# Two fused layers with sorted experts: gather rows, result loads and the order of the second layer's sequences are changed

## The chip, the core and the metric

One core of a Trainium2 chip. Its five engines run their own in-order instruction streams: TensorE (PE, matmuls and transposes into PSUM), VectorE (DVE), ScalarE (ACT), GpSimd (POOL, which here issues the indirect and the accumulating DMAs) and SyncE (SP, which issues the plain DMAs). Sixteen DMA engines move the data of all queues. The metric is the device time of one execution in microseconds (us), the median of several runs.

## The reference

The input `x` is 8 sequences of 1024 tokens with 256 features (float32). Two layers follow each other:

```python
x = L0_attn_x
xn = _layernorm(x, axis=-1)
x = x + _L0_attn_ref(xn, ...) + _L0_ffn_ref(xn, ...)
xn = _layernorm(x, axis=-1)
x = x + _L1_attn_ref(xn, ...) + _L1_ffn_ref(xn, ...)
return x
```

- `_L0_attn_ref` is a linear recurrence with a 16-wide state for each of 256 channels, then a layer norm, a GELU, a product with `W_out`, plus `b_out`, plus its input `xn`.
- `_L0_ffn_ref` is a shared expert plus the two best of 8 experts for each token, each `silu(x Wg) * (x Wu) Wd`, weighted with the token's two gates.
- `_L1_attn_ref` takes its softmax over an axis of length one, so each token gets the sum of the values of its sequence, times `w_o`.
- `_L1_ffn_ref` is 8 experts with two per token and a capacity of 2048 tokens each, hidden width 1024, ReLU.

The sum that layer 0 hands on is, for each token, `x + xn + b_out + shared expert` (called "the other terms" below), plus the two weighted expert results, plus the projection of the recurrence.

## The kernel before

64 tiles of 128 tokens; eight tiles are a sequence. The tile `y` holds all tokens in SBUF. The kernel is written in a framework that adds the semaphores, gives buffers of a pool in turn, and lets a simulated schedule put each engine's instructions in order: a later instruction of the program may be issued earlier on its engine if it is ready then. A buffer goes to its next user when every instruction that reads it, a DMA too, has finished. There are five stages.

**Stage A (0 to 209 us), the shared expert and the router, by pairs of tiles.** `normal` writes the normalized rows into `xr4` (three buffers of four tiles) and SP copies them twice into the DRAM table `xnd`, once for each of the token's two choices: 8192 x 2 rows of 257 numbers. `both` makes on ACT the channel-major copy `xc` (L588) and, in place, `y = x + xn` (L592). `shared` runs the shared expert and adds it to `y` (L617). For each sequence `fill` writes `b_out` to the DRAM table `base` from SP (L535), and POOL adds `y` to it with an accumulating DMA (L655). `route0` finds the two experts and gates of 16 tiles, and SP writes the gates into column 256 of `xnd` (L528).

**Stage B (209 to 346 us), the plan.** Ranks, block starts, and one-hot matmuls (`find`, `found`) that give for each of 142 columns of 128 rows the row of `xnd` to gather (`choice`) and the row of the result table `yr` to scatter to (`goes`).

**Stage C (346 to 862 us), 71 expert blocks of 256 rows beside the recurrence.** `bring(n)` copies the expert's number on POOL (L787), loads its weights into `wb` (three buffers) from SP, and gathers two times 128 rows into `xb` (three buffers, L792). `widen(n)` transposes them and runs the first two products; `narrow(n)` runs the third, scales by the gate (L811) into `yo` (two buffers of its own) and scatters from POOL into `yr` (L814). On POOL's stream a block's two scatters come before the gathers of three blocks later. `krylov` and `rest` are the recurrence, whose output replaces `y`.

**Stage D (862 to 1160 us), by sequences b = 0 to 7.** `load(b)` brings the sum's other terms from `base` into `hb` with a plain DMA and then adds the two expert results to it with two accumulating DMAs from POOL (L952), for b = 0 with plain loads and VectorE. The loop at L1228 loads b + 2, normalizes and turns b + 1 (`turn`: ACT L190, PE L933, GELU L934), projects b (`project`: PE L992, DVE L999 adds `hb`), and finishes b (`finish`: moments, the root, normalized rows `xs`, transposes L1022 and L1025, the DRAM table `xd`, router logits L1037). Every second sequence `route` ranks 16 tiles (the one-hot products end in L1140). `attend(b)` copies column sums on POOL (L1053, `vb`), multiplies them on PE (L1056), stores `y` to the output, and adds the result with an accumulating DMA from POOL (L1063). Within an engine the stream is in order, so an instruction of `attend` that waits holds back what follows it.

**Stage E (1160 to 2081 us), layer 1's experts.** 32 blocks of gathered rows, two products (L1339, L1357), an accumulating scatter to the output (L1369). The change does not touch it.

Of the kernel before, what the change touches and what calls it, by code (L numbers as in the profile page):

```python
# [18 lines left out]
P = 128  # L19
# [5 lines left out]
def kernel(  # L25
# [48 lines left out]
    XW = D + 8  # L74
# [11 lines left out]
    base = dram.tile([NTOK, D], F32, name="base")  # L86

    xnd = dram.tile([2 * NTOK, D + 1], F32, name="xnd")
# [128 lines left out]
    with tc.tile_pool(name="xpool", bufs=1) as xpool, tc.tile_pool(name="mo", bufs=2) as mo, tc.tile_pool(  # L217
# [12 lines left out]
        g0 = xpool.tile([P, 2, NT], F32, name="g0")  # L230
        up = xpool.tile([P, NT], F32, name="up")
        off = xpool.tile([P, NT], F32, name="off")
# [5 lines left out]
        choice = xpool.tile([P, NCOL], I32, name="choice")  # L238
        goes = xpool.tile([P, NCOL], I32, name="goes")
# [16 lines left out]
        def hidden(xT, wb, pgu=None):  # L256
# [12 lines left out]
            hh = mo.tile([P, 2 * P], F32, name="hh")  # L269
            nc.vector.tensor_tensor(hh, pgu[:, 0, :], sg, ALU.mult)  # L270
            nc.vector.tensor_tensor(hh, pgu[:, 1, :], hh, ALU.mult)  # L271
            return hh
# [181 lines left out]
        with tc.tile_pool(name="sh", bufs=1) as sh, tc.tile_pool(name="ld", bufs=2) as ld, tc.tile_pool(  # L454
# [5 lines left out]
            scores = sh.tile([P, NT, E], F32, name="scores")  # L460
            cb_t = sh.tile([P, E], F32, name="cb_t")
# [10 lines left out]
            bout_t = sh.tile([P, D], F32, name="bout_t")  # L472
            nc.scalar.dma_start(bout_t, b_out.partition_broadcast(P))
# [6 lines left out]
            nc.vector.tensor_copy(rwT.rearrange("p c e -> p (c e)"), pr[:, : DC * E])  # L480

            def route0(n, tiles):
# [38 lines left out]
                for k in range(2):  # L521
                    wk = rt.tile([P, n, E], F32, name="wk")
                    nc.vector.tensor_tensor(wk, w, hot[k], ALU.mult)
                    nc.vector.tensor_reduce(g0[:, k, tiles], wk, AX.X, ALU.add)
                    mine = xnd[2 * tiles.start * P : 2 * tiles.stop * P, :].rearrange(
                        "(i p k) c -> k p i c", p=P, k=2
                    )[k]
                    nc.sync.dma_start(mine[:, :, D], g0[:, k, tiles])  # L528
# [4 lines left out]
            def fill(b):  # L533

                nc.sync.dma_start(  # L535
                    base[b * S : (b + 1) * S, :].rearrange("(i p) d -> p i d", p=P),
                    bc(bout_t, 1, [P, TPB, D]),
                )

# [16 lines left out]
            def scale(g, mv):  # L556
# [9 lines left out]
                nc.vector.tensor_scalar(up[:, tiles], rstd, 1.0, None, ALU.add)  # L566
# [4 lines left out]
            def normal(i, mv, rstd):  # L571
# [7 lines left out]
                if i % 4 == 3:  # L579
                    for kk in range(2):  # L580
                        mine = xnd[2 * (i - 3) * P : 2 * (i + 1) * P, :].rearrange(
                            "(i p k) c -> k p i c", p=P, k=2
                        )[kk]
                        nc.sync.dma_start(mine[:, :, :D], rows[i // 4])

            def both(i, rstd):
# [4 lines left out]
                )  # L591
                nc.scalar.activation(  # L592
                    y[:, i, :], y[:, i, :], AF.Identity, bias=off[:, i : i + 1], scale=up[:, i : i + 1]
                )

            def shared(i, pr, rstd):
# [16 lines left out]
                for q in range(2):  # L613
                    both(i + q, rstd[:, q : q + 1])
                pgu = ps_k.tile([P, 2, 2 * P], F32, name="pk") if n % 2 else None
                pd = down(hidden(xT, sw, pgu), sw)
                nc.vector.tensor_tensor(y[:, i : i + 2, :], pd, y[:, i : i + 2, :], ALU.add)  # L617
# [9 lines left out]
            for s, g in enumerate(sets):  # L627
# [8 lines left out]
                for k in range(0, len(g), 2):  # L636
# [5 lines left out]
                    if i % TPB == 0:  # L642
                        pr = ps_y.tile([P, TPB, E], F32, name="py")
                        fill(i // TPB)
# [6 lines left out]
                    if i % TPB == TPB - 2:  # L651
# [3 lines left out]
                        nc.gpsimd.dma_start(  # L655
                            base[b * S : (b + 1) * S, :].rearrange("(i p) d -> p i d", p=P),
                            y[:, tiles, :], accum_op=ALU.add,
                        )
# [253 lines left out]
    with tc.tile_pool(name="xr", bufs=3) as xr, tc.tile_pool(name="tr", bufs=1) as tr, tc.tile_pool(  # L912
# [64 lines left out]
        def turn(b):  # L977

            ys = y[:, b * TPB : (b + 1) * TPB, :]
            if b:  # L980
                normalize_act(ys, ys, *scaled[b], TPB)
# [430 lines left out]
```

## Time and profile before

| what | value |
|---|---|
| runs shown | 2085.64, 2090.27, 2096.55 us; median 2090.27 |
| the profiled execution | 2092.45 us, of which its span is 2090.8 us |
| PE busy | 1858.0 us, 89% of the span |
| DVE, ACT, POOL busy | 696.9, 717.8, 677.9 us |
| mean granted TensorE clock | 0.939 of full |
| moved by DMA | 233.16 MB, mean 112 GB/s |

The span runs from the first to the last instruction. "Busy" is the time in which an engine had an instruction running; a matmul's end is modelled by the profiler, so PE's busy time includes overlap and is not PE at its peak. The "DMA share" of a stretch is the busy share of the 16 DMA engines, and can pass 1 where packets overlap. A wait is put down to the engine or DMA whose signal came last.

### The profile page before, as it was taken

Reading aid. Unit: us, or ns where it says so; the run is one execution under the profiler, and the core shown is the slowest. Engines: PE = TensorE matmul, PEld = TensorE weight load, DVE = VectorE, ACT = ScalarE, POOL = GpSimd, SP = SyncE. Lnnn points to the kernel's source line nnn. Section 1 sums busy time; section 2 is a strip of 40 time slices with the busy share of each in tenths; the row PEclk is TensorE's granted clock in tenths of the full one; section 3 lists DMA queues with packets and bytes.
Section 4 is the critical chain, followed back from the end, with each engine's and each line's share of the span. In section 5 each row is a group of like instructions: output and inputs, shape, how many; then the busy total and the mean of one; then the engine's idle time right before and its main releaser. Section 6 shows DMA issues by size and latency. Waiting matters only on the chain. (4 is left out here: it accounts for less than half of the span.)

```text
span 2090.8 us, 24217 instructions
## 1 busy us (share of the span) xinstructions
PE 1858.0 (89%) x8619; PEld 1398.3 (67%) x8619; DVE 696.9 (33%) x2093; ACT 717.8 (34%) x1626; POOL 677.9 (32%) x688
## 2 busy tenths in 40 slices
PE   6978798989889897767677899999999999999996
PEld 5867586877777776556565466666666666666664
DVE  6754794444443443535556110100111001011000
ACT  5953352222222221545655222222222222222221
POOL 0000003555555566211110333333333333333322
PEclk9988898999999999888887899999999999999998
DMA  9987214545454555699966223232322222232211
GB/s 275 219 190 179 52 47 120 156 145 165 135 153 135 151 177 157 185 249 178 195 129 157 56 39 79 39 76 36 78 40 59 59 59 54 39 79 38 39 20 20
DMA packets 228888, 233.16 MB, mean 112 GB/s; under 512 B 50904, under 2 KB 203296, under 8 KB 228640
## 3 DMA queue, kind: packets, MB, share of 16 engines
q0 software_dynamic: 69408, 102.87, 25.3%
q1 hardware_dynamic: 156672, 126.35, 21.1%
q10 hardware_dynamic: 2688, 2.40, 0.4%
q8 instruction: 68, 1.11, 0.2%
q14 instruction: 52, 0.43, 0.1%
HBM read 136.87 MB, written 97.85 MB: 112 GB/s over the span
## 5 line engine op out<-in xcount | busy, mean ns | idle before, releaser
L1339 PE MATMUL phe<-xTe,w1t 128*128 128x512 f32 x1024 | 447.5, 595 | 0.6 <-issue 0.6
L1357 PE MATMUL poe<-w2t,hT 128*128 128x256 f32 x2048 | 447.3, 379 | 0.0
L1357 PEld LDWEIGHTS poe<-w2t,hT 128*128 128x128 f32 x2048 | 386.7, 190 | 51.7 <-issue 0.5
L1339 PEld LDWEIGHTS phe<-xTe,w1t 128*128 128x128 f32 x1024 | 195.5, 191 | 233.9 <-issue 230.7
L1369 POOL DMA_INDIRECT out_dram<-yo,invi x128 | 201.7, 1576 | 444.7 <-DMA out_dram<-yo,invi 245.6
L1346 ACT ACTIVATE hT<-phe,b1T 128x512 f32<-128x512 f32 x256 | 176.0, 687 | 248.7 <-PE phe L1339 242.5
L1368 ACT ACTIVATE yo<-yo,gr 128x256 f32<-128x256 f32 x128 | 58.0, 500 | 441.4 <-DVE yo L1364 441.4
L1364 DVE TENSOR_TENSOR yo<-poe,b2t 128x512 f32<-128x512 f32 x64 | 44.3, 692 | 406.6 <-PE poe L1357 400.5
L1308 POOL DMA_INDIRECT xg<-xd,invi x128 | 124.1, 969 | 168.1 <-PE px L1322 129.1
L322 PE MATMUL pk<-kr 128*128 128x129 f32 (+7 forms) x896 | 150.9, 306 | 27.3 <-ACT kr L333 24.4
L1323 DVE COPY xTe<-px 128x512 f32<-128x512 f32 x64 | 41.2, 686 | 383.5 <-PE px L1322 383.5
L814 POOL DMA_INDIRECT yr<-yo,goes x142 | 141.9, 1000 | 77.5 <-DVE yo L811 36.3
L322 PEld LDWEIGHTS pk<-kr 128*128 128x128 f32 x896 | 129.5, 202 | 51.7 <-ACT kr L333 35.7
L263 PE MATMUL pgu<-xT,wb 128*128 128x256 f32 x568 | 147.3, 405 | 13.1 <-ACT xT L253 10.4
L792 POOL DMA_INDIRECT xb<-xnd,choice x142 | 141.1, 993 | 46.9 <-issue 36.0
L263 PEld LDWEIGHTS pgu<-xT,wb 128*128 128x128 f32 x568 | 112.0, 203 | 42.5 <-ACT xT L253 21.9
L333 ACT COPY kr<-pk 128x256 f32<-128x256 f32 x192 | 69.4, 374 | 125.2 <-DVE kr L329 92.7
L268 ACT ACTIVATE sg<-pgu 128x256 f32<-128x256 f32 x87 | 33.4, 384 | 199.1 <-PE pgu L263 154.6
L278 PE MATMUL pd<-wb,hh 128*128 128x256 f32 x284 | 84.5, 412 | 12.2 <-DVE hh L271 12.0
L270 DVE TENSOR_TENSOR hh<-pgu,sg 128x256 f32<-128x256 f32 x87 | 36.8, 423 | 152.0 <-ACT sg L268 123.6
L787 POOL COPY wb<-wrow 1x1 int32<-1x1 int32 x71 | 12.9, 182 | 229.9 <-PE pgu L752 117.8
L811 DVE TENSOR_SCALAR yo<-pd,xb 128x256 f32<-128x256 f32 x142 | 62.4, 478 | 51.9 <-PE pd L278 40.1
(319 smaller groups left out, 2424.7 us busy)
## 6 DMA issues: line engine op xcount, KB each, us to landing
wb<-wpk SPq DMA_DIRECT2D x71, 384.0 KB
xnd<-xr SPq DMA_DIRECT2D x32, 512.0 KB
hk<-kscr SPq DMA_DIRECT2D x32, 512.0 KB
hb<-yr POOLq DMA_DIRECT2D x14, 1024.0 KB
base<-bout_t SPq DMA_DIRECT2D x8, 1024.0 KB
base<-y POOLq DMA_DIRECT2D x8, 1024.0 KB
hb<-base SPq DMA_DIRECT2D x8, 1024.0 KB
w1t<-in_L_ffn_w_dram SPq DMA_DIRECT2D x8, 1024.0 KB
```

Source lines behind the costliest of these rows:

```text
L263: nc.tensor.matmul(pgu[:, j, :], lhsT=gu[:, j, c, :], rhs=xT[:, c, :], start=(c == 0), stop=(c == DC - 1),)
L278: nc.tensor.matmul(pd[:, q, :], lhsT=hh[:, q * P : (q + 1) * P], rhs=wb[:, 2 * DC * I : WW], start=True, stop=True,)
L322: nc.tensor.matmul(pk[:, j, :n], lhsT=t[:, 1 - j, P:], rhs=t[:, j, P - k : P - k + n], start=True, stop=True,)
L333: nc.scalar.copy(t[:, :, P:], pk[:, :, k : k + P])
L792: nc.gpsimd.indirect_dma_start(out=xb[:, q, : D + 1], out_offset=None, in_=xnd[:, :], in_offset=bass.IndirectOffsetOnAxis(ap=choice[:, 2 * ...
L811: nc.vector.tensor_scalar(yo[:, q, :], pd[:, q, :], xb[:, q, D : D + 1], None, ALU.mult)
L814: nc.gpsimd.indirect_dma_start(out=next(yr_own)[:, :], out_offset=bass.IndirectOffsetOnAxis(ap=goes[:, 2 * n + q : 2 * n + q + 1], axis=0) ...
L1308: nc.gpsimd.indirect_dma_start(out=xg[:, q, :], out_offset=None, in_=xd[:, :], in_offset=bass.IndirectOffsetOnAxis(ap=invi[:, q0 + q : q0 ...
L1339: nc.tensor.matmul(ph, lhsT=w1t[:, c, h * P : (h + 1) * P], rhs=xT[:, c], start=(c == 0), stop=(c == DC - 1),)
L1346: nc.scalar.activation(hT[:, h], ph, AF.Relu, bias=b1T[:, e * HC + h : e * HC + h + 1])
L1357: nc.tensor.matmul(po[:, r, :], lhsT=hT[:, h, q + r, :], rhs=w2t[:, h, :], start=(h == 0), stop=(h == HC - 1),)
L1369: nc.gpsimd.indirect_dma_start(out=of[:, :], out_offset=bass.IndirectOffsetOnAxis(ap=invi[:, q0 + r : q0 + r + 1], axis=0), in_=yo[:, r, : ...
```

## The change

- `base`, `fill` and their accumulating DMAs go. `xnd` has one row per token, of 514 numbers: the normalized row, the two gates, and half of the sum's other terms. The halves come from `b_out` and `sw_down` times 0.5, `up` times 0.5 and a new column `offh`. `y = x + xn` moves from ACT (L592) to two VectorE instructions per pair of tiles, and the shared expert's result is added by two VectorE instructions of 256 columns instead of one of 512. SP writes the half rows once per four tiles.
- The gather takes the token's whole row (2056 bytes instead of 1028). A new tile `which` says which of the two gates counts; two small VectorE instructions per block (`gk`, `gs`) select it. `narrow` adds the scaled product to the half row inside `xb` and scatters from there; `yo`'s own buffers go. So both expert results of a token carry one half of the other terms each.
- `load` brings both results with two plain DMAs per sequence into `yk` (three buffers of half a sequence); `project` adds them on VectorE, two instructions per pair of tiles instead of one.
- In stage D the loop runs with a lag: in turn b it projects b, and turns out, ranks and attends b - 1. `vb` is copied on VectorE instead of POOL. The last sequence follows behind the loop in two halves.

```diff
-    base = dram.tile([NTOK, D], F32, name="base")
-    xnd = dram.tile([2 * NTOK, D + 1], F32, name="xnd")
+    xnd = dram.tile([NTOK, XR], F32, name="xnd")          # XR = 2 * D + 2
...
-            nc.vector.tensor_tensor(hh, pgu[:, 0, :], sg, ALU.mult)
-            nc.vector.tensor_tensor(hh, pgu[:, 1, :], hh, ALU.mult)
+            nc.vector.tensor_tensor(sg, pgu[:, 0, :], sg, ALU.mult)
+            nc.vector.tensor_tensor(sg, pgu[:, 1, :], sg, ALU.mult)
...
-                    mine = xnd[...]
-                    nc.sync.dma_start(mine[:, :, D], g0[:, k, tiles])
+                nc.sync.dma_start(token_rows(tiles)[:, :, D : D + 2], g0[:, tiles, :])
...
-                    for kk in range(2):
-                        nc.sync.dma_start(mine[:, :, :D], rows[i // 4])
+                    nc.sync.dma_start(mine[:, :, :D], rows[i // 4])
...
-                nc.scalar.activation(
-                    y[:, i, :], y[:, i, :], AF.Identity, bias=off[:, i : i + 1], scale=up[:, i : i + 1]
-                )
...
-                nc.vector.tensor_tensor(y[:, i : i + 2, :], pd, y[:, i : i + 2, :], ALU.add)
+                for t in range(i, i + 2):
+                    nc.vector.scalar_tensor_tensor(
+                        y[:, t, :], y[:, t, :], up[:, t : t + 1], bhalf, ALU.mult, ALU.add
+                    )
+                pd = down(hh, sw)
+                for q in range(2):
+                    nc.vector.scalar_tensor_tensor(
+                        y[:, i + q, :], pd[:, q, :], offh[:, i + q : i + q + 1], y[:, i + q, :],
+                        ALU.add, ALU.add,
+                    )
+                if i % 4 == 2:
+                    nc.sync.dma_start(
+                        token_rows(slice(i - 2, i + 2))[:, :, D + 2 :], y[:, i - 2 : i + 2, :]
+                    )
...
-                        out=xb[:, q, : D + 1],
+                        out=xb[:, q, :XR],
...
+                gk = mo.tile([P, 2, 2], F32, name="gk")
+                nc.vector.tensor_tensor(
+                    gk, xb[:, :, D : D + 2], which[:, 2 * n : 2 * n + 2, :], ALU.mult
+                )
+                gs = mo.tile([P, 2], F32, name="gs")
+                nc.vector.tensor_reduce(gs, gk, AX.X, ALU.add)
...
-                yo = eb_.tile([P, 2, D], F32, name="yo", bufs=2)
+                yo = xb[:, :, D + 2 : XR]
                 for q in range(2):
-                    nc.vector.tensor_scalar(
-                        yo[:, q, :], pd[:, q, :], xb[:, q, D : D + 1], None, ALU.mult
+                    nc.vector.scalar_tensor_tensor(
+                        yo[:, q, :], pd[:, q, :], gs[:, q : q + 1], yo[:, q, :],
+                        ALU.mult, ALU.add,
                     )
...
-            nc.sync.dma_start(hb, base[toks, :].rearrange("(i p) d -> p i d", p=P))
-                for j in range(2):
-                    nc.gpsimd.dma_start(hb, both[:, :, j, :], accum_op=ALU.add)
+            for t in range(0, TPB, TPB // 2):
+                yk = xr.tile([P, TPB // 2, 2, D], F32, name="yk")
+                nc.sync.dma_start(yk, both[:, t : t + TPB // 2])
+                hold[b].append(yk)
...
-                nc.vector.tensor_tensor(ys[:, t : t + 2, :], po, hb[:, t : t + 2, :], ALU.add)
+                nc.vector.tensor_tensor(two, po, yk[:, :, 0], ALU.add)
+                nc.vector.tensor_tensor(two, two, yk[:, :, 1], ALU.add)
...
-            nc.gpsimd.tensor_copy(vb, bc(colsum[:, :, b], 2, [P, DC, P]))
+            nc.vector.tensor_copy(vb, bc(colsum[:, :, b], 2, [P, DC, P]))
...
         for b in range(NB):
+            project(b)
+            if b + 1 < NB:
+                load(b + 1)
+            nc.sync.dma_start(of[...], y[:, b * TPB : (b + 1) * TPB, :])
+            last = b - 1
+            if b:
+                normal_out(last, whole)
+            if b + 1 < NB:
+                normal_in(b + 1)
+            if b:
+                turn_out(last, whole)
+            if b + 1 < NB:
+                turn(b + 1)
+            if b < NB - 1:
+                measure(b, whole)
+                if b:
+                    logits(last)
+                roots(b)
+            else:
+                measure(b, slice(0, TPB // 2))
+                logits(last)
+            if b:
+                attend(last)
+            if b and last % 2 == 1:
+                ends = route((last - 1) * TPB, 2 * TPB, ends)
```

`normal_out`, `turn_out` and `logits` are the parts of the old `finish`, `normal_in` the first half of the old `turn`; `roots` takes the root and the reciprocals of both norms and starts the moments of sequence b + 3.

## The prediction

> **What bounds the kernel now.** The chain of waits says PE for the end, but follows back only to 1134 us: it shows stage E, 921 us of products without a pause, which the change leaves alone. So I took busy time by stages (us; PE, PEld, DVE, ACT, POOL busy with counts; clock; DMA share; GB/s):
>
> ```profile
> 20.00:72.00 52.00, 50.34 (x314) 45.47 (x314) 39.76 (x168) 48.06 (x105) 1.79 (x1) 1.00 0.96 295
> 72.00:121.00 49.00, 47.86 (x280) 42.11 (x279) 39.02 (x145) 44.09 (x80) 4.66 (x3) 1.00 0.99 208
> 121.00:209.00 88.00, 69.97 (x320) 58.52 (x320) 40.64 (x127) 32.53 (x74) 6.20 (x4) 0.79 0.83 192
> ...
> 346.00:862.00 516.00, 450.58 (x2553) 378.84 (x2551) 219.90 (x642) 134.25 (x352) 289.57 (x348) 0.95 0.49 146
> 862.00:1160.00 298.00, 207.80 (x1107) 168.85 (x1107) 154.84 (x522) 162.29 (x404) 44.38 (x47) 0.81 0.86 190
> 1160.00:2081.00 921.00, 912.32 (x3322) 610.60 (x3322) 90.68 (x160) 233.99 (x384) 319.29 (x250) 0.99 0.26 51
> ```
>
> Stage A starts full on PE and on DMA, then PE thins out. Stage C is 87% PE with POOL at 56%. Stage D has no engine over 70% and a DMA share of 0.86. The waits of stage D (engine and line, whom it waited for, us, times, longest):
>
> ```profile
> POOL hb L952 <- DMA hb<-yr: 83.4, 6, 19.1
> DVE y L999 <- PE pd L992: 58.1, 5, 21.3
> ...
> POOL hb L952 <- DMA hb<-base: 41.4, 4, 18.5
> ```
>
> and POOL's timeline in it (start, duration, then in brackets the idle time before):
>
> ```profile
> 928.02 1.55 POOL L952 DMA_DIRECT2D hb<-yr  x1 [2.73 <-DVE colsum L1045]
> 928.91 1.07 POOL L1053 COPY vb<-colsum 128x256 f32<-128x256 f32 x1
> 949.06 1.55 POOL L952 DMA_DIRECT2D hb<-yr  x1 [19.08 <-DMA hb<-yr]
> ```
>
> Each accumulating load takes 18 to 20 us to land, the second of a sequence waits for the first, and POOL waits in order. So a sequence costs two of them, about 37 us, and 298 / 8 is 37.3: stage D runs at their pace. PE suffers through `vb` (L1053), which stands behind them on POOL: the products of `attend` wait for it, and the next projection waits behind those.
>
> Stage A's late stalls, on PE's timeline:
>
> ```profile
> 150.66 1.10 PE L278 MATMUL pd<-sw,hh 128*128 128x256 f32 x4 [1.21 <-DVE hh L271]
> 158.76 1.22 PE L249 MATMUL pt<-ident,xr 128*128 128x128 f32 x4 [7.00 <-DVE xr L576]
> ```
>
> PE is idle 7 us for normalized rows. DVE makes eight `xr` rows in one burst at 125.8 and six at 158.3, having had gaps up to 7.3 us just before: rows wait for the buffers of `xr4`, and those for their DMAs, in a queue that is full (share 0.96 and 0.99 until 121).
>
> **Stage A, forecast -28 us.** The router's products L606 (8 per pair of tiles) number 72, 90 and 96 in the first three windows: 9, 11 and 12 pairs, at 49 / 11.25 = 4.4 us per pair in the second and 88 / 12 = 7.3 in the third. Removed are 8 fills and 8 accumulating transfers of 1 MB and four of eight gate writes. The second copy of the normalized rows is replaced by the half rows, 16 DMAs of 512 KB for 16. The 45 MB of the stage become 28; the first 121 us alone moved 25. So I expect no DMA stall. Then VectorE counts. Per pair it gains two instructions from SBUF and two from PSUM, 256 wide (0.42 by L576 and L270), and loses one of 0.69 (L617): +1.0 on 39.0 / 11.25 = 3.5, so 4.5, just over PE's pace of 4.4. I take 4.7 per pair. The last 12 pairs gain 12 x 2.6 = 31 and the 11 before them lose 0.3 each: 28 net. ACT loses two of 0.59 (L592) per pair; it is hidden behind PE. Ends: -35 (pace kept at 4.4), -10 (VectorE at 6.2).
>
> **Stage B, nothing.** `found` gains two instructions of 142 columns, under 0.3 us each; the first gathers wait for it, so at most 0.6 us.
>
> **Stage C, forecast +10 us.** Three edits. (1) The gate: 71 x 2 small VectorE instructions of about 0.17 (the smallest rows), 24 us on an engine with 296 us free; if they delayed `narrow`, it would be 0.34 per block. (2) 142 gathers of twice the bytes, +18.7 MB in a stage of half-busy DMA engines. Gathers run three blocks ahead, so a us or two of landing is hidden. (3) The new wait, the one that speaks against the change: the scatter now reads `xb`, so the gather of block n + 3 can be issued only when block n's scatters have landed. Behind it on POOL stand the next expert copy and the next scatters, and through them all later gathers. A block on POOL with no wait:
>
> ```profile
> 616.28 0.18 POOL L787 COPY wb<-wrow 1x1 int32<-1x1 int32 x1
> 616.63 1.01 POOL L814 DMA_INDIRECT yr<-yo,goes  x1 [0.17 <-issue]
> 617.94 0.98 POOL L814 DMA_INDIRECT yr<-yo,goes  x1 [0.30 <-issue]
> 619.23 1.01 POOL L792 DMA_INDIRECT xb<-xnd,choice  x1 [0.30 <-issue]
> 620.54 0.97 POOL L792 DMA_INDIRECT xb<-xnd,choice  x1 [0.30 <-issue]
> ```
>
> That is 5.2 us; with the usual 0.58 after the copy 5.6. The stage needs 516 / 71 = 7.3 per block. The trace's DMA packets tell the landing: the stage's last scatter, undisturbed, was there 1.1 us after its instruction, all 142 in the median 2.0, nine in ten within 2.8. With 2.0 in place of the gap of 0.3 a block is 7.3, exactly the pace. As blocks come unevenly (5.2 to 12.3 us between scatters) and three buffers smooth only part, I take +10. A rule weighs here: the Trainium skill, "DMA: Bandwidth & Descriptors", section "Anatomy of one DMA", gives a fixed 2.0 us per GpSimd DMA, mostly the write's receipt, plus bytes / 436 GB/s; 128 KB make 2.3 from the issue, or 1.3 after the 1.0 of the instruction. By it a block is 6.6 and the wait costs nothing. I follow the row, which has this stage's traffic. Ends: 0, and at 2.8 us 71 x 0.8 = +57.
>
> **Stage D, forecast -47 us.** Gone are 14 accumulating loads from POOL and the loads of `base`; what comes instead is one MB per DMA from SP. The first sequence's plain loads, made today, show the price: 3 MB issued at 861.4 to 863.7 were added up from 870.2 to 875.5, about 4 us per MB. The new loads go out when a half buffer is free, a turn ahead, so they hide; uncovered they would cost 8 us per sequence. On SP they stand behind the store of `xd` and of the router's weights, both of the turn before. POOL keeps only L1063, for which nobody waits until stage E.
>
> What is late next is PE: 207.8 / 8 = 26.0 us per sequence. ACT has 162.3 / 8 = 20.3. DVE has 154.8, less L961 (4.9), plus 32 second adds of 0.69 and eight `vb` copies of 0.4: 175 / 8 = 21.9. The lag lets PE turn b - 1 while b's moments are made, where it now waits (36.3 us in stage D before L1022). Full overlap of three engines so near each other is not to be had: I take 29 per turn. Sum: 5 to the first product (2 MB to load instead of 3), 16 for turn 0 (projection 7.1, moments 6.3, root 2.5), 6 x 29 = 174, 7 for the last projection, 5 for what of sequence 6 now comes behind it (L1037 and L1056), and today's 42 from the last L999 (1119.9) to the first L1339 (1161.8), which still holds the last halves and the routing. That is 249, against 300 today with the same ends; I round the gain of 51 down to 47 for the last loop turn's moments.
>
> The second rule: the Trainium skill, "TensorE: Matmul & The Clock Gate", Part 1, says the clock is gated by default and recent activity releases it. Stage D stands at 0.81. By the rule a denser stage gets 1.00, PE falls to 21 per sequence, VectorE leads, a turn is 25 and the stage gains 24 more. By the row I grant nothing, since PE still pauses in each turn. Ends: -71 and, at a turn of 34, -17.
>
> **Sum.** -28 + 10 - 47 = -65 against the profiled execution's 2092.45 (1.7 beyond its span): 2027.5. That run lies 2.2 above the median of those shown. I write 2028.
>
> **Rivals.**
> 1. The forecast: near 2028; 55%.
> 2. The chain in D goes but another takes its place, at 34 us per turn: SP in order (a half load behind the store of `out`, which waits for the whole projection) or VectorE, which gains 2.5 per sequence and feeds PE in both directions. With A at -12 and C at +10: 2092 - 12 + 10 - 17 = 2073. For it: three engines near 22 to 26 and in-order queues. Against it: none is over 70% today. 21%.
> 3. The other side: the landing in C decides. From 3.0 us a block on POOL is 8.3 and the stage costs 71 x 1.0 = +71, which eats all; at 3.6 it is 8.9 and +114, so 2092 - 28 - 47 + 114 = 2131. For it: POOL's order, the doubled gathers on the same engines, and that one landing in ten is already 2.8. Against it: the median, and that the schedule may put the next scatter before the gather. 18%.
> 4. The traffic is less and the stalls stay (A's wait for rows is not the queue but the order on SP, D's loads collide with the stores): within 0.5% of 2090; 6%.
>
> Differences within 0.5%, some 10 us, can't be told from no change here. Faster: cases 1 and 2, 0.76. Same: 0.06. Slower: 0.18. The range runs from 1985 (A -35, C 0, D -71) to 2095, which leaves case 3 out.
>
> **What would show it.** Right: no L952 on POOL and `pd` starting every 27 to 31 us in D; in A PE's gaps for `xr` gone and the last router product near 180; in C two us of idle POOL before the gathers and a stage of about 525. Wrong: POOL idle 3 us or more there with a stage over 570 (case 3); D over 280 with PE waiting for `yk` or for VectorE (case 2); A still with bursts of `xr`.

## The result, and the profile after

The changed kernel is slower. Its time is 2149.06 us (median of 4 runs, 2139.66 to 2152.03) against 2091.16 of the kernel before on the same chip (4 runs): ratio 1.027, 95% interval 1.023 to 1.031. The profiled execution has a span of 2145.1 us against 2090.8, so the two profiles differ by 54.3 us. To see where, I cut both by the same events: the end of the last router product (A), the first scatter (B), the last scatter (C), the first product of layer 1's experts (D), the end (E).

| stage, us | before | changed | difference | forecast |
|---|---|---|---|---|
| A, to the last router product | 200.5 | 214.1 | +13.6 | -28 |
| B, to the first scatter | 148.1 | 149.8 | +1.7 | 0 |
| C, to the last scatter | 509.7 | 623.1 | +113.4 | +10 |
| D, to the first product of stage E | 303.5 | 229.2 | -74.3 | -47 |
| E, to the end | 929.0 | 928.9 | -0.1 | 0 |

The differences add up to the 54.3. (Some of the expectations below give stage A from the record's zero, 10.5 us earlier: 211.0 and 224.6 there are 200.5 and 214.1 here.) Busy time by stages of the changed kernel, in the columns of the prediction's first view (PE, PEld, DVE, ACT, POOL; clock, DMA share, GB/s):

```profile
20.00:72.00 52.00, 50.01 (x311) 45.21 (x309) 42.42 (x166) 34.44 (x75) 0.00 (x0) 1.00 0.64 210
72.00:121.00 49.00, 29.84 (x152) 24.52 (x152) 36.59 (x141) 30.14 (x52) 0.00 (x0) 0.84 0.45 117
121.00:209.00 88.00, 76.82 (x379) 65.68 (x379) 58.59 (x201) 24.20 (x48) 0.00 (x0) 0.86 0.39 104
364.00:987.00 623.00, 485.73 (x2521) 395.45 (x2519) 224.43 (x756) 128.99 (x344) 287.83 (x345) 0.90 0.51 149
987.00:1216.00 229.00, 184.84 (x1129) 160.30 (x1128) 172.31 (x576) 165.53 (x412) 21.18 (x29) 0.87 0.79 212
1216.00:2138.00 922.00, 911.64 (x3320) 610.30 (x3320) 89.93 (x159) 233.99 (x384) 320.11 (x250) 0.99 0.27 50
```

Three things are to be seen. In A the DMA share fell from 0.96 and 0.99 to 0.64 and 0.45, as forecast, and PE still stands: 29.8 of 49 us busy. In C every engine is busy for a smaller share of the stage than before, so the stage waits for something. In D the same products keep PE busy for 184.8 us instead of 211.5, with a granted clock of 0.87 instead of 0.80. Stage D in the kernel before, cut by the same events:

```profile
858.00:1162.00 304.00, 211.51 (x1126) 171.98 (x1126) 155.93 (x525) 164.90 (x409) 47.21 (x52) 0.80 0.85 188
```

The waits of stage C in the changed kernel (engine and line, whom it waited for, us, times, longest); L794 is the gather, L808 the gate's first instruction `gk`, L246 the transposes of the gathered rows, L274 the third product:

```profile
POOL xb L794 <- issue: 124.4, 87, 5.7
POOL xb L794 <- DMA yr<-xb,goes: 122.1, 34, 5.8
...
POOL wb L789 <- issue: 8.4, 7, 2.0
...
DVE gk L808 <- DMA xb<-xnd,choice: 239.4, 65, 8.2
...
PE pt L246 <- DMA xb<-xnd,choice: 58.3, 44, 3.2
PE pd L274 <- DVE sg L267: 36.4, 22, 4.5
```

In the kernel before they were (346 to 862 us; L792 is the gather, L249 the transposes):

```profile
POOL wb L787 <- issue: 111.4, 47, 8.5
...
POOL xb L792 <- issue: 34.7, 114, 0.3
...
PE pt L249 <- DMA xb<-xnd,choice: 2.8, 4, 1.4
```

POOL stands 247 us ahead of gathers, where before it stood some 40 in this stage; half is put down to the landing of the scatters, the other half ("issue") is the same wait, made by an instruction of its sequencer. The 111 us that POOL had to spare before, ahead of the copy of the expert's number (`wb`), have shrunk to 8. VectorE stands 239 us ahead of `gk`, which did not exist before. PE waits for rows (58 us, before 3) and for VectorE's products (36 us). POOL's timeline shows the first of these waits (start, duration, idle time before in brackets):

```profile
651.29 1.01 POOL L824 DMA_INDIRECT yr<-xb,goes  x1 [0.17 <-issue]
652.60 0.99 POOL L824 DMA_INDIRECT yr<-xb,goes  x1 [0.30 <-issue]
657.22 0.99 POOL L794 DMA_INDIRECT xb<-xnd,choice  x1 [3.63 <-DMA yr<-xb,goes]
658.52 0.97 POOL L794 DMA_INDIRECT xb<-xnd,choice  x1 [0.30 <-issue]
```

The gather stands right behind the scatter whose landing it needs, and starts 3.6 us after it; before, the gap at this place was 0.3. VectorE's timeline shows the second:

```profile
646.99 0.88 DVE L820 SCALAR_TENSOR_TENSOR xb<-pd,gs,xb 128x256 f32<-128x256 f32 x2 [2.17 <-DMA yr<-xb,goes]
653.77 0.16 DVE L808 TENSOR_TENSOR gk<-xb,which 128x4 f32<-128x4 f32 x1 [5.90 <-DMA xb<-xnd,choice]
653.85 0.28 DVE L295 TENSOR_TENSOR kr<-a_in,mask 128x128 f32<-128x128 f32 x1
...
654.18 0.41 DVE L266 TENSOR_TENSOR sg<-pgu,sg 128x256 f32<-128x256 f32 x1
```

As soon as one block's sums are made (646.99), VectorE's next instruction is the gate of the following block. It takes 0.16 us and waits 5.9 us for that block's rows, and behind it in order stand an instruction of the recurrence and the products of the blocks.

### The profile page after: what moved, and what is told of

Its sections match the earlier page's. It is cut to its first block, busy times and chain, and to the rows that moved or that the text cites. A ratio compares the mean times of both kernels' runs of the same rounds, so it can differ in the third digit from the quotient of the medians.

```text
span 2145.1 us, 24245 instructions
## 1 busy us (share of the span) xinstructions
PE 1872.7 (87%) x8619; PEld 1408.8 (66%) x8619; DVE 748.6 (35%) x2373; ACT 688.9 (32%) x1566; POOL 639.8 (30%) x658
## 3 DMA queue, kind: packets, MB, share of 16 engines
q8 instruction: 68, 1.11, 0.2%
## 5 line engine op out<-in xcount | busy, mean ns | idle before, releaser
L794 POOL DMA_INDIRECT xb<-xnd,choice x142 | 141.2, 995 | 256.7 <-issue 125.7
L824 POOL DMA_INDIRECT yr<-xb,goes x142 | 141.7, 998 | 75.8 <-DVE xb L820 33.5
L260 PEld LDWEIGHTS pgu<-xT,wb 128*128 128x128 f32 x568 | 117.1, 210 | 34.3 <-ACT xT L250 13.4
L274 PE MATMUL pd<-wb,sg 128*128 128x256 f32 x284 | 96.2, 461 | 36.7 <-DVE sg L267 36.4
L246 PE MATMUL pt<-ident,xb 128*128 128x128 f32 x284 | 58.4, 310 | 66.1 <-DMA xb<-xnd,choice 61.3
L265 ACT ACTIVATE sg<-pgu 128x256 f32<-128x256 f32 x87 | 33.5, 385 | 208.8 <-PE pgu L260 196.1
L808 DVE TENSOR_TENSOR gk<-xb,which 128x4 f32<-128x4 f32 x71 | 11.6, 163 | 248.2 <-DMA xb<-xnd,choice 243.2
```

Source lines behind the costliest of these rows:

```text
L246: nc.tensor.transpose(pt[:, c, q * P : (q + 1) * P], src[:, q, c * P : (c + 1) * P], ident)
L260: nc.tensor.matmul(pgu[:, j, :], lhsT=gu[:, j, c, :], rhs=xT[:, c, :], start=(c == 0), stop=(c == DC - 1),)
L274: nc.tensor.matmul(pd[:, q, :], lhsT=hh[:, q * P : (q + 1) * P], rhs=wb[:, 2 * DC * I : WW], start=True, stop=True,)
L794: nc.gpsimd.indirect_dma_start(out=xb[:, q, :XR], out_offset=None, in_=xnd[:, :], in_offset=bass.IndirectOffsetOnAxis(ap=choice[:, 2 * n + ...
L824: nc.gpsimd.indirect_dma_start(out=next(yr_own)[:, :], out_offset=bass.IndirectOffsetOnAxis(ap=goes[:, 2 * n + q : 2 * n + q + 1], axis=0) ...
```

## The experiments

The kernel before took 2111, 2110, 2111 and 2091 us in the four sets of runs below (2091 in the first comparison), on several chips, one of which gave both 2110 and 2091, while the changed kernel stayed at 2145 to 2149. So an edit is judged by the stages of its profile, and by ratios within a set; a ratio from one of the first three sets would be about 0.01 higher against 2091. Stage C of the changed kernel repeated to 0.2 us, that of the kernel before to 3.3, but kernels with the changed kernel's stage C and an edit elsewhere came to 617.6 to 628.2: differences of some 5 us in stage C mean nothing.

Stage A is less steady: kernels that have it exactly as in the changed kernel came to 213.7 to 223.1. From 10 us to the last router product PE is idle for 39 to 40 us in all of them; what differs is its busy time for the same 879 products, 164.2 us at a granted clock of 0.90 up to 173.6 at 0.86. In the kernel before PE is idle for 27.1 us there. So a change of stage A is read below from PE's idle time, and its busy time is given beside it.

| run | ratio to before (95%) | A | B | C | D |
|---|---|---|---|---|---|
| changed, again | 1.016 (1.013 to 1.019) | 217.7 | 148.4 | 622.9 | 231.3 |
| c_own_yo | 1.010 (1.007 to 1.014) | 213.7 | 156.1 | 584.9 | 240.8 |
| c_late_gate | 1.018 (1.014 to 1.022) | 223.0 | 146.5 | 624.6 | 227.6 |
| b_yo_in_xb | 1.031 (1.027 to 1.035) | 201.1 | 147.9 | 595.5 | 303.6 |
| c_behind | 1.029 (1.025 to 1.033) | 222.6 | 146.4 | 643.8 | 228.8 |
| c_pin | 1.009 (1.006 to 1.012) | 222.6 | 146.4 | 602.3 | 229.7 |
| c_pin_yo | 0.986 (0.982 to 0.990) | 223.1 | 156.3 | 545.5 | 238.9 |
| c_pin_xc | 0.977 (0.972 to 0.982) | 216.2 | 149.5 | 529.9 | 230.8 |
| c_pin_xc_size | 0.973 (0.969 to 0.976) | 214.5 | 147.7 | 522.6 | 229.6 |
| a_order | 1.017 (1.014 to 1.021) | 213.9 | 146.8 | 617.6 | 228.3 |
| a_act | 1.008 (1.005 to 1.011) | 196.1 | 148.8 | 628.2 | 228.7 |
| d_nolag | 1.043 (1.039 to 1.046) | 215.2 | 148.3 | 619.3 | 288.9 |
| best3 | 0.969 (0.967 to 0.972) | 198.9 | 148.9 | 526.2 | 228.2 |
| before, again | one run, 2091.04 us | 199.8 | 147.6 | 506.4 | 306.3 |

### Stage C: the landing alone, and its removal

**The wait alone, in the kernel before.** The product goes into `xb` and is scattered from there; nothing else of the change is in.

```diff
-                yo = eb_.tile([P, 2, D], F32, name="yo", bufs=2)
+                yo = xb[:, :, :D]
```

> The kernel before with one edit: the scaled product is written into xb's first 256 columns (dead after the transposes) and scattered from there; nothing else of the change. Theory L: stage C grows from 511 to about 511 + 71 x (5.6 + 3.1 - 0.3 - 7.3) = 590 (its landing is 2.0 and the notice 1.15 us), the time to about 2091 + 80 = 2170, within 2155 to 2195. Theories G and S (no gate instructions, no doubled rows here): within 15 of 2091.

Stage C took 595.5 us against the 590 expected, 86 more than before, and every other stage stayed. The waits of that stage:

```profile
POOL xb L792 <- DMA yr<-xb,goes: 129.9, 34, 6.0
POOL xb L792 <- issue: 127.1, 81, 5.3
...
PE pt L249 <- DMA xb<-xnd,choice: 108.0, 81, 5.8
```

POOL's 257 us before the gathers are here without gate and doubled rows. So the landing is a cause, enough by itself to make the stage 17% longer. The records of the DMA packets, worked out for the first gather of each block from the fourth on and for the last scatter ahead of it, say what the wait is made of (us, 10th, 50th and 90th percentile, mean):

```
changed kernel, 68 gathers
scatter's end -> gather's start        2.21  3.51  4.62   3.40
scatter's end -> its last DMA packet   1.09  2.34  3.19   2.24
last DMA packet -> gather's start      1.11  1.15  1.24   1.16
```

The packets land as the forecast had read it (2.0 there); then another 1.15 us pass, nearly constant, until the waiting gather starts.

**The wait away, in the changed kernel.** The sum goes into the tiles of `woutT` and `wvo`, whose weights are then made behind the last block.

```diff
-                yo = xb[:, :, D + 2 : XR]
+                yo = (woutT, wvo)[n % 2]
...
-                        yo[:, q, :], pd[:, q, :], gs[:, q : q + 1], yo[:, q, :],
+                        yo[:, q, :], pd[:, q, :], gs[:, q : q + 1], xb[:, q, D + 2 : XR],
```

> The changed kernel with one edit in stage C: the scatter reads buffers of its own again (the tiles of woutT and wvo, unused until stage D, whose weights are then made behind the last block), so a gather need not wait for a landing; row size, gate and stages A and D as changed. Theory L (the gather waits for the scatter's landing, 3.4 us from the scatter's end to the gather's start, on POOL's loop): stage C falls from 624 to about 520 and the time to about 2149 - 105 = 2044, POOL's idle time before the gathers from 257 to under 60. Theory S (the doubled row is what slows the stage): the gain is under 30, above 2119. Theory G (VectorE stands in order behind the gate's small instructions): gains what L says only because the rows then land early; the gate-late run tells the two apart.

POOL's wait before the gathers fell to 41 us, what it was before, and stage C only to 584.9 instead of 520; the time, 2128.6, lies where the doubled row was to leave it (above 2119). VectorE still stood 159 us ahead of `gk` between 370 and 840 us (195 in the changed kernel). The landing is not the only cause; the gate and the doubled row are told apart below.

**The gather one block later** (`issue_after` fixes an engine's order without adding a wait):

```diff
+                with tc.issue_after(scattered[0]):
                     for q in range(2):
                         nc.gpsimd.indirect_dma_start(
                             out=xb[:, q, :XR],
```

> The changed kernel with each gather put one block later on POOL's stream, behind the scatters of the next block, so that the scatters it waits for have long landed; two blocks of rows are gathered ahead instead of three. Theory L: POOL's wait goes, and with a lead of two blocks the rows are mostly there: stage C about 530 to 560, the time 2060 to 2090. If instead the lead of three is what the stage needs, PE waits for rows and the time stays above 2120.

It went the other way: 643.8 us. POOL no longer waits for a landing, and PE waits for rows in nearly every block. The waits between 370 and 840 us:

```profile
PE pt L246 <- DMA xb<-xnd,choice: 101.8, 71, 5.1
...
POOL yr L826 <- DVE xb L822: 103.1, 49, 5.1
```

With rows gathered only two blocks ahead, the gather waits for a scatter, the scatter for the sum, the sum for the products of rows gathered just before. So the lead of three is what the stage needs, and a later start of the gathers, by a landing too, eats into it. (The gate's wait is in this run as well, so its 643.8 is not the price of the shorter lead alone.)

### Stage C: the gate

**A late gate, as I first wrote it.** `gk` and `gs` moved from `widen` to `narrow` in the program.

> The changed kernel with gk and gs made in narrow, just ahead of the scaled sum, instead of in widen. Theory G (the 243 us that VectorE spends ahead of gk hold back the recurrence and the next products): gains 70 or more, to 2080 or below. Theory L: POOL's loop of 5.6 + 3.4 - 0.3 = 8.7 us per block stays, so stage C stays above 600 and the time within 25 of 2149.

Stage C did not move (624.6), and the wait was still there:

```profile
DVE gk L813 <- DMA xb<-xnd,choice: 217.5, 59, 7.3
```

This says nothing against the gate: in the schedule `gk` depends on the gathered rows alone, so it had been put ahead of its block's products again, and VectorE's stream was nearly the same as before the edit. The edit must hold the order:

```diff
+                with tc.issue_after(made_hidden[0]):
                     gk = mo.tile([P, 2, 2], F32, name="gk")
```

> The changed kernel with gk and gs held behind their own block's second product (sg) on VectorE's stream; the late-gate run did not do this, since the schedule put gk ahead of the block's products again. The scatter still reads xb. Theory now: two causes, POOL's wait for the landing (8.4 to 8.7 us per block) and VectorE's wait in order for the next block's rows ahead of gk. With the second gone stage C stays at the first's pace, about 595 as in the run of before with the product in xb (623 with both), so the time is about 1.013 of before. If only the landing counts: no gain, 1.027. If only the gate counts: stage C under 540, below 0.99.

Stage C took 602.3, close to the 595 named and 21 less than in the changed kernel, and VectorE no longer waits at `gk`. What is left is the landing, which PE now meets itself:

```profile
PE pt L246 <- DMA xb<-xnd,choice: 113.9, 67, 5.4
```

**Both away.**

> As the run with held gates, and the scatter reads its own buffers (woutT and wvo). Both causes gone: stage C 515 to 530 against before's 510, the time (2145 - 100) / 2091 = 0.978 of before. If the doubled rows or the added VectorE work cost by themselves, stage C stays above 560 and the ratio above 0.995.

Stage C took 545.5: 39 us less than with the buffers alone, 57 less than with the held gate alone. It stayed above the 530 named for two causes and below the 560 named for the doubled rows, and stages B and D were 7 and 10 us longer, with the weights moved behind the last block. So the sums went elsewhere, into four buffers in columns of `xc` that the recurrence has finished with by then, and the weights back:

```diff
-                yo = xb[:, :, D + 2 : XR]
+                yo = dead[n % 4]
```

> Both causes in stage C removed as in the run with held gates and own buffers, but the scattered rows lie in columns of xc that the recurrence has finished with (four buffers), so the weights of stage D are made where they were. If the 36 us that were left in stage C came from the moved weights and from two buffers: stage C 515 to 530, ratio 0.975 to 0.98. If from the doubled rows: stage C about 545 again, B and D 8 each less, ratio about 0.98.

Stage C took 529.9, B and D were as in the changed kernel, and the whole is faster than before (0.977). Whether the moved weights or the two buffers had cost the 16 us between the two runs is not told apart. Its waits in stage C:

```profile
POOL xb L800 <- issue: 34.9, 114, 0.4
...
PE pt L246 <- DMA xb<-xnd,choice: 12.2, 12, 2.0
```

**The row size.** The gather brings 258 numbers instead of 514; the halves of the other terms are left out of the results.

> As the run with rows in xc's columns, but the gathers bring only the row and its gates, 258 numbers instead of 514, and the halves of the other terms are left out of the results. Theory size (the doubled gathers land later and slow the expert weights' loads): stage C 510 to 520, 20 or more below the run with full rows. Theory order (what is left is VectorE's added work and the schedule): within 8 of it.

522.6 us, 7 less. The run does not isolate the size: as the sum no longer reads `xb`, its buffers come free earlier, and the schedule put the gathers four blocks ahead instead of three. And best3 below, whose stage C is the same as in the run with full rows, took 526.2 instead of 529.9. So the doubled rows cost 7 us at most by this run, far less than either wait, and it is not shown that they cost anything. The stage then still lies 16 above the 506.4 of before's second profile; VectorE's added instructions are the likely rest, which no run isolates.

### Stage A

ScalarE's timeline in the changed kernel has 14 channel copies in a row ahead of the copy `xT` (L250) that PE needs, and PE's timeline the wait for it:

```profile
111.68 8.43 ACT L582 ACTIVATE xc<-y,off,rstd 128x256 f32<-128x256 f32 x14
119.93 0.61 ACT L250 COPY xT<-pm 128x512 f32<-128x512 f32 x1
...
120.59 1.88 PE L597 MATMUL py<-rwT,xT 128*128 128x8 f32 x8 [7.52 <-ACT xT L250]
```

So I first held each pair's channel copies behind its `xT`:

```diff
+                with tc.issue_after(turned[0]):
                     for q in range(2):
                         channels(i + q, rstd[:, q : q + 1])
```

> The changed kernel with one edit in stage A: on ScalarE's stream the channel copies xc of a pair of tiles come behind that pair's xT copy; in the changed kernel up to 14 of them (8.4 us) stand ahead of an xT copy for which PE waits. Theory ACT order: the last router product comes 20 to 30 us earlier (at 224.6 in the changed kernel), near 200, and PE's wait for xT (13.8) falls under 5; ratio 1.013 to 1.018. Rival VectorE: its 39 instructions of 256 columns more per stage set the pace at 4.7 us per pair or more, and the product comes within 6 us of where it was; ratio 1.025 or more.

The wait for `xT` went (13.0 to 0.9 us between 72 and 209 us), and PE's idle time stayed at 39.2 us and the last router product at 213.9, since another wait took its place two pairs of tiles later on PE's timeline:

```profile
128.25 1.99 PE L248 MATMUL pm<-ident,xr 128*128 128x128 f32 x8 [11.01 <-DVE xr L575]
```

The ratio, 1.017, is what the first theory had named, but the changed kernel itself came to 1.016 in another set, so it tells nothing here.

Next the added VectorE work itself was taken away; the half of `b_out` is left out of the halves here.

```diff
-                    nc.vector.scalar_tensor_tensor(
-                        y[:, t, :], y[:, t, :], up[:, t : t + 1], bhalf, ALU.mult, ALU.add
-                    )
+                    nc.scalar.activation(
+                        y[:, t, :], y[:, t, :], AF.Identity,
+                        bias=offh[:, t : t + 1], scale=up[:, t : t + 1],
+                    )
...
+                nc.vector.tensor_tensor(y[:, i : i + 2, :], pd, y[:, i : i + 2, :], ALU.add)
```

> The changed kernel with stage A's y = x + xn back on ScalarE and one VectorE addition of 512 columns per pair, as before; the half of b_out is left out of the halves. VectorE loses 1.16 us per pair, 37 in the stage. Theory VectorE (rows come late because its in-order stream carries more): the last router product comes near 200 (224.6 in the changed kernel, 211.0 before), ratio 0.01 below the changed kernel's. Theory ACT order or DMA: within 6 of 224.6.

Stage A took 196.1 against 217.7 of the changed kernel in the same set. VectorE's busy time in it fell by 25 us (142.0 to 116.6); PE's idle time fell by 10.7 us (40.3 to 29.6), and the other 10.9 are its busy time for the same products (167.4 to 156.5), at a granted clock of 0.93 instead of 0.88. Of PE's waits those for rows are left, now with a DMA share of 0.42 to 0.67 (between 72 and 209 us):

```profile
PE pm L246 <- DVE xr L573: 7.8, 2, 6.7
PE pt L246 <- DVE xr L573: 7.0, 1, 7.0
```

The same stall of 7.0 us is in the kernel before, in a stretch with a DMA share of 0.83. It is VectorE's order that makes it, not the queue: on VectorE's timeline of the kernel before, the router's small instructions for 16 tiles (`route0`) stand without a pause from 152.4 us up to the rows for which PE waits,

```profile
158.10 0.28 DVE L524 TENSOR_REDUCE g<-wk 128x16 f32<-128x128 f32 x1
158.30 2.02 DVE L576 TENSOR_SCALAR xr<-y,mv,rstd 128x256 f32<-128x256 f32 x6
```

and in the run without the added work they stand ahead of the rows at both stalls of 7 us.

### Stage D without the lag

The old order of the loop, with the new loads and with `vb` on VectorE.

> The changed kernel with the loop of stage D in the old order (projects b, turns b + 1 in, then measures, normalizes, turns out, ranks and attends b in the same turn), with the new plain loads and vb on VectorE. Stage D took 303.5 before and 229.2 after. Theory chain: the plain loads alone bring it, within 15 of 229. Theory lag: a sequence is then projection 7.1, moments 6.3, root 2.5, normalized rows, turning and logits one after the other, about 32 us, and stage D 250 to 275, ratio 1.037 to 1.05.

Stage D took 288.9, above even the 250 to 275 named: without the lag the new loads and `vb` on VectorE bring 15 us of the 74, the lag on top of them the other 60. Busy time of the stage (first line) and PE's waits in it:

```profile
983.00:1272.00 289.00, 214.05 (x1123) 174.28 (x1123) 174.02 (x577) 166.79 (x409) 21.61 (x29) 0.78 0.62 169
...
PE pi L1160 <- ACT hh L1158: 24.3, 6, 8.6
PE pt L1040 <- ACT xs L189: 19.2, 11, 4.2
```

With the lag, in the changed kernel, the same two waits are

```profile
PE pi L1160 <- ACT hh L1158: 6.0, 2, 3.9
...
PE pt L1040 <- ACT xs L189: 3.8, 3, 2.6
```

From the first start of a projection to the last it is 35.2 us per sequence before, 32.9 without the lag, 21.7 with it. So the loads' chain of 37 us per sequence stood beside a second one of nearly the same length, the steps of one sequence one after the other, and the lag undoes that one. What the lag would bring with the accumulating loads still there was not run. Part of the gain comes back at the end: from the start of the last projection to the first product of stage E it is 49.1 us before and 70.9 in the changed kernel, since the work of the last sequence follows behind the loop.

### A version that beats both

Both waits of stage C away, and stage A relieved with nothing left out: `y = x + xn` on ScalarE, the half of `b_out` added on GpSimd.

```diff
+                nc.gpsimd.tensor_tensor(
+                    y[:, i : i + 2, :], y[:, i : i + 2, :], bc(bhalf, 1, [P, 2, D]), ALU.add
+                )
```

> The changed kernel with stage C's two waits removed (gates held behind their block's products, scattered rows in columns of xc) and stage A relieved of VectorE work with nothing left out: y = x + xn on ScalarE, the half of b_out added on GpSimd, which is idle there, the expert's product added by one VectorE instruction. If GpSimd's additions don't slow VectorE: the last router product near 207 to 212 (226.6 without), stage C 530, the time 2035 to 2045, ratio 0.965 to 0.97 of before. If the two get into each other's way: stage A as it was, ratio 0.975 to 0.98.

2025.62 us (5 runs, 2021.95 to 2032.73) against 2091.35: ratio 0.969, interval 0.967 to 0.972. Stage A took 198.9 (PE idle for 30.5 us of it from 10 us on), C 526.2, D 228.2. Computed in full, it shows that VectorE's work and not the left-out term was the cause in stage A. With it ran:

> The kernel before itself, for a profile on this chip, where its runs take 2111 instead of 2091. If its stage C takes 525 to 530 here, then nothing is left to explain in stage C once both waits are gone (529.9); if 510, some 13 us remain for VectorE's added instructions and the doubled rows besides the 7 that the rows alone showed.

Stage C of the kernel before took 506.4, so some 20 us are left in stage C once both waits are gone, at most 7 of them the doubled rows. What made the kernel before 2110 us in three sets stays open, since no profile of it was taken there.

> The changed kernel itself, so that the edits can be compared with it on one chip; no theory is asked. Its ratio was 1.027 (1.023 to 1.031) at first; on the chip of the later runs between 1.017 and 1.027.

It came to 1.016 (1.013 to 1.019): by the set, the changed kernel is 1.6 to 2.7% slower.

## Why the prediction was wrong

It named 2028 us in a range of 1985 to 2095, and the time was 2149. (The slow ends of its own stages, -10, +57 and -17, add up to 2122, so 2095 was narrower than its working.) Step by step:

- **Stage C, edit (3), is the step that failed.** The wait itself was seen: the gather stands directly behind its scatters, and each block pays L - 0.3 more on POOL. L was mis-sized. The forecast read it off the DMA packets as 2.0, which was nearly so (2.24 in the mean), but the waiting gather does not start with the last packet. It started 1.16 us later, so L is 3.4. That alone made +86 us in b_yo_in_xb, where +10 was forecast for the whole stage. The loop around it was a little too long: of its 5.6 us the 0.4 beyond the row's 5.2 were slack between the copy and the scatter, and it shrank to the row's 0.17 where POOL set the pace. With 5.2 the sum fits where the landing stands alone (L of 3.57: 5.2 + 3.57 - 0.3 = 8.47 for the measured 8.49 in b_yo_in_xb; L of 3.66: 8.56 for 8.59 in c_pin); in the changed kernel it gives 8.3, and the mean period was 8.88, the rest being the gate's. Rival 3 gave +114 for this stage at L = 3.6, and the stage grew by 113: the wait was the right one, the match is partly luck, since L was 3.4 and part of the 113 is the gate's. The row that was missing can be had from any wait on a DMA: start of the waiting instruction minus end of the last packet. The rule of the Trainium skill, "DMA: Bandwidth & Descriptors", section "Anatomy of one DMA", would have been further off: the estimate from it was 1.3 from the instruction's end, and 3.4 was measured.
- **Stage C, "Gathers run three blocks ahead, so a us or two of landing is hidden"** was wrong with it: once the gather waits for a landing, the lead is what is lost; PE's wait for rows went from 3 us to 108 in b_yo_in_xb.
- **Stage C, edit (1), failed too.** "24 us on an engine with 296 us free" prices two small instructions by their duration. What counts is what they wait for and who stands behind them. The gate's place costs 21 us beside the landing (623.1 to 602.3) and 39 without it (584.9 to 545.5); the landing costs 38 beside the gate (623.1 to 584.9) and 57 without it (602.3 to 545.5; 72 with the sums in `xc`). With both present each hides part of the other.
- **Stage A was wrong in sign.** The step that failed is "rows wait for the buffers of `xr4`, and those for their DMAs". The gap of 7.3 us on VectorE stands behind the burst of 125.8, not ahead of one, and ahead of the burst of 158.3 VectorE has no gap: it works at the router. So less traffic could not remove that stall. The share of the DMA engines fell as forecast, and without the added VectorE work PE is idle for 29.6 to 30.5 us, where it was 27.1 before: no idle time was won where 31 us were named, and the 2 to 4 us by which the stage is shorter then (198.9 and 196.1 against 200.5) lie in PE's busy time. The VectorE term was named and too small: its added work costs 9 to 11 us of PE's idle time and, with the busy time at another clock, 17 us (216.2 to 198.9) to 22 us (217.7 to 196.1).
- **Stage B**: +1.7, at most 0.6 was named; kernels that leave the stage alone came to 146.4 to 149.8, so this is not clear of the spread.
- **Stage D was right in direction and too small.** It had 29 us per turn; it is 21.7. The forecast refused the faster clock of the Trainium skill, "TensorE: Matmul & The Clock Gate", Part 1, because PE pauses in each turn. With that rule the forecast was -71, and -74 was measured, but this is partly luck: the rule's clock was 1.00 and its turn 25, the profile has 0.87 and 21.7, and the end from the last projection's start took 70.9 us where the forecast has 7 + 5 + 42 = 54. PE's busy time fell by 27 us with the same products, so to grant no faster clock at all was wrong. The weight of the parts was mistaken too: the accumulating loads were named as the pace, and their removal without the lag gave 15.
- **Stage E**: right.

The 2028 is near what the chip gives with both causes in C and the one in A removed (2026), but its parts are others: A -2, C +17, D -75 there, -28, +10 and -47 in the forecast. The change's idea holds; its waits cost more than it gains.

## What to carry to other kernels

When a buffer is freed by a DMA instead of by an engine, count from the end of the issuing instruction to the start of the waiting one (3.4 us here), not to the last packet (2.2), and ask which lead that wait consumes. A small instruction in an in-order stream costs what it waits for, as far as others that could run stand behind it: give it a place behind its own block's work, and look at the stream afterwards, since moving the line in the program need not move it there. Before a stall is put down to a full queue, look whether the engine that is waited for was itself the late one; and where a stage has one chain at its pace, look for the second chain of nearly the same length.

## What was not expected of the hardware

- From a scatter's last DMA packet to the start of the gather that waits for it pass 1.11 to 1.24 us (10th to 90th percentile) in the changed kernel, 1.11 to 1.29 in b_yo_in_xb and 1.12 to 1.25 in c_pin, while the time to that packet goes from 1.1 to 4.1 us in the three.
- GpSimd's additions (1.31 us in the mean, 32 of them) slowed some of VectorE's instructions that read and write SBUF alone: the normalized rows took 540 ns in the mean and up to 1441, against 403 without GpSimd. By the trace it is the 19 of 64 that overlap an addition, 843 ns in the mean; the other 45 kept 403. Four of the router's small instructions went from 290 to as much as 1124. The moments (L549, L551), which read and write SBUF too, kept their time, and so did the sums that read PSUM. The groups of VectorE between 20 and 200 us (busy us, mean ns), of a_act:

```profile
L573 DVE TENSOR_SCALAR xr<-y,mv,rstd 128x256 f32<-128x256 f32 x62 | 22.1, 403 | 0.0
L614 DVE TENSOR_TENSOR y<-pd,y 128x512 f32<-128x512 f32 x31 | 21.3, 688 | 16.7 <-PE pd L274 16.3
L549 DVE BATCH_NORM_STATS2 st<-y 128x6 f32<-128x256 f32 x56 | 21.1, 406 | 0.0
```

and of best3:

```profile
L575 DVE TENSOR_SCALAR xr<-y,mv,rstd 128x256 f32<-128x256 f32 x61 | 30.2, 540 | 0.0
L551 DVE BATCH_NORM_STATS2 st<-y 128x6 f32<-128x256 f32 x56 | 21.1, 405 | 0.0
L619 DVE TENSOR_TENSOR y<-pd,y 128x512 f32<-128x512 f32 x30 | 20.7, 689 | 16.8 <-PE pd L276 16.5
```

The longest is about 1.0 us longer than usual, less than one GpSimd addition, as if VectorE waited for its end; that it does is not shown. Stage A still gained.

- The granted clock differed between stages of the same products: 0.80 for stage D before, 0.78 without the lag, 0.87 with it, and 29 us of PE's busy time between the last two (214.1 and 184.8). The denser stage has the higher clock; that its fewer pauses are the reason is not isolated here.
